# One core, attention over block sums with a residual layer norm: engine orders from a list schedule, and a projection of values

## The chip, the cores and the metric

The kernel runs on one core of a Trainium2 chip. The core has five engines, each with a queue of its own that it works through in order: TensorE (PE: matmuls; PEld: its weight loads), VectorE (DVE), ScalarE (ACT), GpSimd (POOL) and SyncE (SP, which here issues transfers). They meet only at semaphores. SBUF is the working memory of 128 partitions, PSUM the memory that TensorE writes; GpSimd has only operands in SBUF here. The metric is the time of one execution in microseconds; lower is better.

## The reference

`x` is 8 x 512 x 1024 in float32 (batch, sequence, hidden). The sequence of each batch is cut into 8 blocks of 64 rows.

```python
block_repr = inputs.reshape(B, n_blocks, block_size, H).sum(axis=2)
keys = jnp.einsum('bnh,kh->bnk', block_repr, Wk)
rms = jnp.sqrt(jnp.mean(keys * keys, axis=-1, keepdims=True) + EPS)
keys = keys / rms * rms_weight
scores = jnp.einsum('bnh,h->bn', keys, q)
attn = jax.nn.softmax(scores, axis=-1)
attended = jnp.einsum('bn,bnh->bh', attn, block_repr)
attended = jnp.broadcast_to(attended[:, None, :], (B, S, H))
proj = jnp.einsum('bsh,kh->bsk', attended, Wo)
x = inputs + proj
mu = jnp.mean(x, axis=-1, keepdims=True)
var = jnp.mean((x - mu) ** 2, axis=-1, keepdims=True)
out = (x - mu) / jnp.sqrt(var + EPS) * ln_gamma + ln_beta
...
x = x + _L0_cond_ref(...)
```

There are 8 x 8 blocks to attend over, one projected vector per batch, and then 4096 rows to be normalised and added to their input.

## The kernel before

**Tiles.** The 8 batches are taken as four groups of two (`GROUPS`). A group has 1024 rows of `x`, held as 8 "rows" of 128 x 1024 (one sequence row per partition), two to a tile of 1 MB, so that there are 32 rows `k` and 16 tiles in all. 13 tile buffers (`XBUFS`) hold `x` and, at first, the weights: SyncE issues group 0's four tiles, four of Wk, four of Wo, and then `x` tiles as buffers come free (L86, L95). TensorE transposes the weights into `wkT` and `woT` (L191), ScalarE and VectorE copying out in turn.

**The chain of a group.** `block_sums` (L222) adds the 64 rows of each block by matmuls with a 0/1 matrix; `to_columns` (L232) transposes the sums into `blkT`. `attend` (L246) makes the keys (`project`, L209: 64 instructions), their squares on ScalarE (L255) and dot products with the query on VectorE (L257), puts both into diagonal form (L260) and sums them over partitions (`pc`, L263). Some fifteen operations of 128 x 16 or 128 x 2 elements follow, nearly all in SBUF: the inverse root by an exponential of a logarithm and one Newton step (L276 to L278), the softmax (L279 to L290), and the weighted sum of the block columns (`att`, L294). `proj` (L300) then multiplies `att` by Wo (`po`, L214 again), adds gamma and beta as two further vectors, copies to `pr`, makes the table `tab` (L316, L319), and `spread_out` (L323) broadcasts the projection over the partitions into `pb` (L327), which has one PSUM buffer of two banks. All other steps of the chain share one PSUM buffer, `s1`.

**The rows.** `y_row` (L343): VectorE adds `pb` to the row in place and gets its sum (L351); ScalarE squares it and gets the sum of squares (L356). For each unit of four rows, `unit_std` (L361, ScalarE, two small operations), `unit_scale` (L368, VectorE, four operations of 128 x 4 elements, L373 to L376) and `unit_stat` (L379: GpSimd fills `stat`, L382; TensorE transposes it, L388; ScalarE copies it to `lt`, L392). `scale_row` (L395): ScalarE makes `A` = 1 + gamma x rs (L398, two buffers), GpSimd multiplies the row by it in place (L399); this document calls that a product. `rest_of_pair` (L401): TensorE makes for two rows what is still to be added, `b` (L411), from `lt` and `tab`. `out_of_pair` (L416): VectorE adds `b` (L420), and SyncE stores the tile and issues the next load.

**The order.** Every queue has the order in which the code emits. Group 0's chain comes first, with the weights' transposes. Then one loop runs over the rows `k`: `y_row(k)`, six rows behind it (`LAG`) `scale_row` and `rest_of_pair`, at each unit's end the unit's steps, eight rows behind `out_of_pair`; at the end of each turn the chains of the later groups, written as generators, are advanced by three pieces (`STEPS`). When a group's first row comes up, what is left of its chain is emitted at once.

## Time and profile before

| | us |
|---|---|
| median of three runs | 245.38 |
| lowest and highest run | 242.53, 247.69 |
| the profiled execution | 243.71 |
| its span in the trace | 241.8 |

The span runs from the first to the last instruction that the trace shows; the execution's own time is 1.9 us longer. The rows quoted below give start and duration in us from the span's start, the engine, the line (L) of the kernel, the output and input by name, and in brackets how long the engine had been idle and what released it. A granted clock (PEclk) of 1.00 is TensorE's level of 2.4 GHz, 0.50 that of 1.2 GHz.

### The profile page before, as it was taken

To read this page: it belongs to the slowest core of one execution; us is meant where nothing else is said; L and a number is where in the kernel's file an instruction comes from. 1 tells how busy PE (TensorE), PEld (TensorE's weight loads), DVE (VectorE), ACT (ScalarE), POOL (GpSimd) and SP (SyncE) were. 2 spreads that over 40 slices of the span, in tenths; PEclk is the share of its full clock that TensorE was granted. 3 is DMA by queue.
4 is the path that set the end of the run, shared out by engine and by line. 5 is a ranking of instruction groups with operands and counts; after the bars stand their busy time and mean duration, and the time that the engine had idled before them with its cause. 6 is when DMAs were issued, how large, how long until landed. Compare 5 with 4: busy or idle time off the path is not lost. (4 is left out here: it accounts for less than half of the span.)

```text
span 241.8 us, 2960 instructions
## 1 busy us (share of the span) xinstructions
PE 139.2 (58%) x1136; PEld 68.4 (28%) x1136; DVE 121.9 (50%) x209; ACT 97.1 (40%) x161; POOL 83.5 (35%) x75
## 2 busy tenths in 40 slices
PE   0677795986159609821578539801597065472970
PEld 0237674543123404301143313301144021211210
DVE  0004547064550154836990282737971595969542
ACT  0204324165370144642462232742371478482520
POOL 7300000000043043244325043433334439386990
PEclk9999999999556977965569756965569755555555
DMA  7999999899000003572454004120403034061664
GB/s 225 396 411 411 407 418 377 274 422 426 20 3 0 0 0 164 186 263 85 174 176 174 0 3 174 64 110 0 174 27 150 0 161 186 0 283 68 251 270 174
DMA packets 7342, 42.93 MB, mean 178 GB/s; under 512 B 792, under 2 KB 1056, under 8 KB 3232
## 3 DMA queue, kind: packets, MB, share of 16 engines
q1 hardware_dynamic: 6784, 41.95, 43.5%
q10 hardware_dynamic: 544, 0.80, 1.0%
q8 instruction: 9, 0.15, 0.2%
q14 instruction: 5, 0.04, 0.0%
HBM read 25.96 MB, written 16.78 MB: 177 GB/s over the span
## 5 line engine op out<-in xcount | busy, mean ns | idle before, releaser
L399 POOL TENSOR_TENSOR x<-x,A 128x1024 f32<-128x1024 f32 x32 | 74.8, 2356 | 94.2 <-ACT A L398 94.2
L351 DVE SCALAR_TENSOR_TENSOR x<-x,pb 128x1024 f32<-128x1024 f32 x32 | 38.2, 1214 | 37.4 <-PE pb L327 37.4
L356 ACT ACTIVATE sq<-x,ysum 128x1024 bf16<-128x1024 f32 x32 | 36.7, 1146 | 37.4 <-DVE x L351 30.6
L411 PE MATMUL b<-tab,lt 4*128 4x512 f32 x128 | 41.6, 949 | 12.6 <-DVE x L420 9.7
L420 DVE TENSOR_TENSOR x<-x,b 128x1024 f32<-128x1024 f32 x32 | 37.8, 1216 | 5.9 <-POOL x L399 4.8
L398 ACT ACTIVATE A<-gam,rs 128x1024 f32<-128x1024 f32 x32 | 36.3, 1137 | 4.0 <-POOL x L399 4.0
L388 PE MATMUL pl<-ident,stat 128*128 128x128 f32 x16 | 5.5, 448 | 50.2 <-POOL stat L382 50.2
L214 PE MATMUL po<-woT,att 128*32 128x256 f32 x256 | 21.5, 497 | 15.0 <-DVE att L294 15.0
L227 PE MATMUL bs<-x,blk 128*32 128x256 f32 x256 | 23.5, 526 | 10.2 <-DMA x<-in_x_dram 8.9
L373 DVE TENSOR_SCALAR ssq<-ssq 128x4 f32<-128x4 f32 x8 | 14.5, 1815 | 21.6 <-ACT r L364 21.6
L411 PEld LDWEIGHTS b<-tab,lt 4*128 4x128 f32 x128 | 12.4, 260 | 32.7 <-DVE x L420 22.0
L382 POOL TENSOR_TENSOR stat<-ysum,rs 128x8 f32<-128x8 f32 x8 | 1.7, 208 | 56.4 <-DVE rs L376 56.4
L214 PEld LDWEIGHTS po<-woT,att 128*32 128x32 f32 x256 | 10.2, 140 | 29.1 <-issue 24.0
L388 PEld LDWEIGHTS pl<-ident,stat 128*128 128x128 f32 x16 | 2.3, 204 | 56.0 <-POOL stat L382 56.0
L199 PE MATMUL pt<-ident,w 128*128 128x128 f32 x128 | 15.6, 275 | 2.5 <-DMA w<-in_L_cond_Wk_dram 1.9
L214 PE MATMUL keys<-wkT,blkT 128*32 128x256 f32 x256 | 15.1, 381 | 1.6 <-DVE blkT L242 1.6
L227 PEld LDWEIGHTS bs<-x,blk 128*32 128x32 f32 x256 | 9.6, 144 | 22.3 <-issue 6.9
L199 PEld LDWEIGHTS pt<-ident,w 128*128 128x128 f32 x128 | 13.9, 141 | 4.3 <-issue 3.0
L392 ACT COPY lt<-pl 128x256 f32<-128x256 f32 x8 | 3.0, 372 | 27.8 <-PE pl L388 27.8
L214 PEld LDWEIGHTS keys<-wkT,blkT 128*32 128x32 f32 x256 | 7.7, 110 | 8.4 <-DVE blkT L242 2.3
L242 DVE COPY blkT<-pblk 128x256 f32<-128x256 f32 x4 | 1.7, 425 | 15.8 <-PE pblk L239 15.8
L327 PE MATMUL pb<-pr,spread 128*128 128x256 f32 x32 | 8.7, 420 | 0.0
(69 smaller groups left out, 97.7 us busy)
## 6 DMA issues: line engine op xcount, KB each, us to landing
x<-in_x_dram SPq DMA_DIRECT2D x16, 1024.0 KB, 5.3
out_dram<-x SPq DMA_DIRECT2D x16, 1024.0 KB, 3.9
w<-in_L_cond_Wk_dram SPq DMA_DIRECT2D x4, 1024.0 KB
w<-in_L_cond_Wo_dram SPq DMA_DIRECT2D x4, 1024.0 KB, 17.7
gam<-in_L_cond_ln_gamma_dram ACTq DMA_DIRECT2D x1, 512.0 KB
qw<-in_cond_dram ACTq DMA_DIRECT2D x4, 32.0 KB, 3.6
w_t<-n_L_cond_rms_weight_dram ACTq DMA_DIRECT2D x4, 32.0 KB
gb<-in_L_cond_ln_gamma_dram ACTq DMA_DIRECT2D x4, 1.0 KB
```

The lines of the kernel that those rows point to most:

```text
L199: nc.tensor.transpose(pt[:, c, r * P : (r + 1) * P], stage[which, s][:, r, bass.ts(4 * h4 + c, P)], ident)
L214: nc.tensor.matmul(po[32 * j : 32 * j + 32, :], lhs(c), wT[:, c, bass.ts(j, QU)], start=(c == 0), stop=(end and c == HC - 1),)
L227: nc.tensor.matmul(G["bs"][32 * j : 32 * j + 32, :], blk[G["g"]], G["x"][t][:, r, bass.ts(j, QU)], start=(t == 0 and r == 0), stop=(t == G ...
L327: nc.tensor.matmul(pb[:, j, :], spread[G["g"]][:, j, :], G["pr"], start=True, stop=True)
L351: nc.vector.scalar_tensor_tensor(x_row(k), x_row(k), 1.0, place[k][0]["pb"], ALU.mult, ALU.add, accum_out=U["sum"][:, i : i + 1])
L356: nc.scalar.activation(junk, x_row(k), AF.Square, bias=U["sum"][:, i : i + 1], scale=-float(H), accum_out=U["ssq"][:, i : i + 1],)
L373: nc.vector.tensor_scalar(ssq, ssq, 1.0 / H**3, EPS, ALU.mult, ALU.add)
L388: nc.tensor.transpose(pl[:, k, :], st[:, RT * k : RT * k + RT].rearrange("p r i k -> p (r i k)"), ident)
L398: nc.scalar.activation(A, gam, AF.Identity, bias=1.0, scale=units[u]["rs"][:, i : i + 1])
L399: nc.gpsimd.tensor_tensor(x_row(k), x_row(k), A, ALU.mult)
L411: nc.tensor.matmul(bb[r][:, i, :], lt[lo : lo + K, :], G["tab"][lo : lo + K, :], start=True, stop=True)
L420: nc.vector.tensor_tensor(x_row(k + r), x_row(k + r), flat(bb[r]), ALU.add)
```

## The change

- **Order.** All work is entered as steps of a plan, each with its engine, an assumed cost, the steps it needs, a rank, and the buffer that it takes or gives back. When all are entered, `Plan.emit` lays them out in time: of all steps whose needs are laid out it takes the one that can start first (ties by rank, lower first), and at last emits all in the order of planned starts. Ranks are: loads -500, Wk transposes -300, small steps on TensorE for the rows -250, chains -200 + group, Wo transposes -199.8, a unit's small steps -150, rows by their number.
- **Units** have 2, 2, 4, 4, 4, 4, 4, 4, 2 and 2 rows. Small per-unit tiles have ten buffers.
- **Values.** The block columns themselves are multiplied by Wo (`values`, in the PSUM buffer `s2`, which the units' `pl` use too), which needs no softmax. The softmax's weights go into `w4` (ScalarE, 128 x 512) and, negative, into `stat`; `spread` multiplies `w4` by the values to make `pb`. `att`, `wb` and the addition over blocks on VectorE go. `b` takes 32 rows of `lt` and `tab` where it took four.
- **The softmax** keeps most of its small operands in the PSUM tile `pc`; the diagonal form on VectorE goes, `pc` being made from the broadcast sums and the diagonal matrix. The reciprocal keeps its operands in SBUF.
- **Units' small steps.** The inverse root (`e_scale`) moves from VectorE to GpSimd, as five operations; the copy to `lt` moves from ScalarE to VectorE.
- **Transfers.** gamma and beta are loaded early, on ScalarE's queue, in three transfers where there were nine. Constants made at the start change with the rest.

The core of the diff:

```diff
 XBUFS = 13
-LAG = 6
-STEPS = 3
+ABUFS = 2
+UNITS = (2, 2, 4, 4, 4, 4, 4, 4, 2, 2)
+class Plan:
+    def emit(self):
+        done, free, dma, start = {}, {}, 0.0, {}
+        pool = {kind: [0.0] * n for kind, n in self.buffers.items()}
+        left = list(range(len(self.steps)))
+        while left:
+            best = None
+            for i in left:
+                engine, cost, _, needs, rank, _, takes, _ = self.steps[i]
+                if any(n not in done for n in needs) or (takes and not pool[takes]):
+                    continue
+                at = free.get(engine, 0.0)
+                if takes:
+                    at = max(at, min(pool[takes]))
+                for n in needs:
+                    at = max(at, done[n] + (0.0 if self.steps[n][0] == engine else self.HOP))
+                if best is None or (at, rank, i) < best:
+                    best = (at, rank, i)
+            at, _, i = best
+            engine, cost, _, _, _, moved, takes, gives = self.steps[i]
+            free[engine] = done[i] = at + cost
+            if moved:
+                dma = max(dma, done[i]) + moved * self.MB
+                done[i] = dma + self.LAND
+            if takes:
+                pool[takes].remove(min(pool[takes]))
+            if gives:
+                pool[gives].append(done[i] + self.HOP)
+            start[i] = at
+            left.remove(i)
+        self.start, self.done = start, done
+        for i in sorted(start, key=lambda i: (start[i], i)):
+            self.steps[i][2]()
...
+    def load_x(G, t, needs):
+        def emit():
+            xx = xp.tile([P, RT, H], F32, tag="x", name=f"x{G['n']}_{t}")
+            nc.sync.dma_start(out=xx, in_=G["x_v"][t])
+            G["x"][t] = xx
+        G["loaded"][t] = plan.add(SP, 0.35, emit, needs, rank=-500 + len(loads), moved=1.0)
+        loads.append(G["loaded"][t])
...
+    def load_vectors():
+        for k, v in ((GAM, gamma), (BET, beta)):
+            dst = gb.rearrange("(j m) k -> j m k", m=32)
+            nc.scalar.dma_start(out=dst[:, k, :], in_=v.rearrange("(j k) -> j k", j=4))
+        nc.scalar.dma_start(out=gam, in_=gamma.rearrange("(o h) -> o h", o=1).to_broadcast([P, H]))
+    vectors = plan.add(ACT, 1.2, load_vectors, [staged[0, 0]], rank=-400)
...
+        def e_pc():
+            T["pc"] = ps.tile([P, 4, 32], F32, tag="s1", name=f"pc{n}")
+            for s in range(2):
+                nc.tensor.matmul(
+                    T["pc"][:, s, :], T["sd"][:, s : s + 1].to_broadcast([P, P]), diag4, start=True, stop=True
+                )
+        def e_ln():
+            T["r"] = row("cr")
+            nc.scalar.activation(T["r"], T["pc"][:, 0, :NB], AF.Ln, bias=eps_t, scale=1.0 / H)
+            nc.scalar.activation(T["r"], T["r"], AF.Exp, scale=-0.5)
+        def e_score():
+            r, pc = T["r"], T["pc"]
+            v, dot, t, a = (pc[:, i, :NB] for i in range(4))
+            nc.vector.scalar_tensor_tensor(t, v, H * EPS, r, ALU.add, ALU.mult)
+            nc.vector.scalar_tensor_tensor(a, t, -0.5 / H, r, ALU.mult, ALU.mult)
+            T["a"] = row("ca")
+            nc.vector.scalar_tensor_tensor(T["a"], a, 1.5, r, ALU.add, ALU.mult)
+            nc.vector.tensor_tensor(t, T["a"], dot, ALU.mult)
+            by = t.rearrange("p (b n) -> p b n", n=NBLK)
+            mx = small.tile([P, g], F32, tag=f"mx{g}", name=f"mx{n}")
+            nc.vector.tensor_reduce(mx, by, AX.X, ALU.max)
+            nc.vector.tensor_tensor(by, by, mx.unsqueeze(2).to_broadcast([P, g, NBLK]), ALU.subtract)
+        def e_exp():
+            nc.scalar.activation(T["pc"][:, 2, :NB], T["pc"][:, 2, :NB], AF.Exp)
...
+        def e_share():
+            sc = T["pc"][:, 2, :NB]
+            by = sc.rearrange("p (b n) -> p b n", n=NBLK)
+            es = small.tile([P, g], F32, tag=f"es{g}", name=f"es{n}")
+            nc.vector.tensor_reduce(es, by, AX.X, ALU.add)
+            nc.vector.reciprocal(es, es)
+            nc.vector.tensor_tensor(by, by, es.unsqueeze(2).to_broadcast([P, g, NBLK]), ALU.mult)
+            T["own"] = small.tile([P, 1], F32, tag="own", name=f"own{n}")
+            junk3 = row("junk3")
+            nc.vector.scalar_tensor_tensor(
+                junk3, sc, 1.0, diag4[:, :NB], ALU.mult, ALU.mult, accum_out=T["own"]
+            )
+        def e_stat0():
+            v = stat[n % 2].rearrange("p r i m -> p (r i) m")[:, :, :NB]
+            nc.vector.tensor_tensor(
+                v, T["pc"][:, 2, :NB].unsqueeze(1).to_broadcast([P, 2 * UNIT, NB]),
+                hide[g].rearrange("p b n -> p (b n)").unsqueeze(1).to_broadcast([P, 2 * UNIT, NB]), ALU.mult,
+            )
+        def e_w4():
+            T["w4"] = chain.tile([P, 4, P], F32, tag="w4", name=f"w4{n}")
+            nc.scalar.activation(flat(T["w4"]), flat(weigh[g]), AF.Identity, scale=T["own"])
+        i = plan.add(ACT, 0.6, e_sq, [keys], rank)
+        i = plan.add(DVE, 0.5, e_dot, [i], rank)
+        i = plan.add(PE, 0.4, e_pc, [i], rank)
+        i = plan.add(ACT, 0.45, e_ln, [i], rank)
+        i = plan.add(DVE, 1.2, e_score, [i], rank)
+        i = plan.add(ACT, 0.22, e_exp, [i], rank)
+        share = plan.add(DVE, 0.8, e_share, [i], rank)
+        G["stat0"] = plan.add(DVE, 0.3, e_stat0, [share, free.get(f"stat{n % 2}")], rank + 0.5, gives="s1")
+        w4 = plan.add(ACT, 0.59, e_w4, [share, free.get("w4")], rank)
+        T["values"] = {}
+        i = project(
+            rank + 0.5, columns, woT, "s2", f"values{n}", [blkT, *ready[1]], T["values"], False, "s2"
         )
-        yield
-
...
+        def e_spread():
+            pb = ps.tile([P, 4, QU], F32, tag="pb", name=f"pb{n}")
+            for j in range(4):
+                nc.tensor.matmul(pb[:, j, :], T["w4"][:, j, :], T["val"], start=True, stop=True)
+            G["pb"] = flat(pb)
...
+        i = plan.add(PE, 0.46, e_gb, [i, vectors], rank + 0.5)
+        free["blkT"] = i
+        val = plan.add(ACT, 0.37, e_val, [i, free.get("val")], rank + 0.5, gives="s2")
+        i = plan.add(PE, 1.1, e_ptab, [val], rank + 0.7, takes="s2")
+        G["tab"] = plan.add(ACT, 0.59, e_tab, [i, free.get(f"tab{n % 2}")], rank + 0.7, gives="s2")
+        G["spread"] = free["w4"] = free["val"] = plan.add(PE, 1.9, e_spread, [val, w4, *pb_free], rank)
...
+        def e_scale():
+            r0, ssq = U["r0"][:, :N], U["ssq"][:, :N]
+            a = unit.tile([P, UNIT], F32, tag="a", name=f"a{u}")[:, :N]
+            U["rs"] = unit.tile([P, UNIT], F32, tag="rs", name=f"rs{u}")
+            nc.gpsimd.tensor_scalar(ssq, ssq, 1.0 / H**3, EPS, ALU.mult, ALU.add)
+            nc.gpsimd.tensor_tensor(a, r0, r0, ALU.mult)
+            nc.gpsimd.tensor_tensor(a, a, ssq, ALU.mult)
+            nc.gpsimd.tensor_scalar(a, a, -0.5, 1.5, ALU.mult, ALU.add)
+            nc.gpsimd.tensor_tensor(U["rs"][:, :N], a, r0, ALU.mult)
+        def e_stat():
+            U["st"] = stat[G["n"] % 2]
+            nc.gpsimd.tensor_tensor(
+                U["st"][:, :N, :, GAM], U["sum"][:, :N].unsqueeze(2).to_broadcast([P, N, 2]),
+                U["rs"][:, :N].unsqueeze(2).to_broadcast([P, N, 2]), ALU.mult,
             )
...
+        std = plan.add(ACT, 0.48, e_std, squares, -150)
+        scale = plan.add(POOL, 1.0, e_scale, [std], -150)
+        i = plan.add(POOL, 0.2, e_stat, [scale, G["stat0"]], -150, takes=st_)
+        i = free[st_] = plan.add(PE, 0.35 * N // RT, e_pl, [i], -250, takes="s2", gives=st_)
+        lt = plan.add(DVE, 0.42, e_lt, [i], -150, takes="lt", gives="s2")
...
+                i = plan.add(ACT, 1.05, e_A, [scale], k, takes="A")
+                vs.append(plan.add(POOL, 2.36, e_v, [i], k, gives="A"))
...
+            bi = free[f"tab{G['n'] % 2}"] = plan.add(
+                PE, 1.5, e_b, [lt, G["tab"], *b_first], -250, takes="b", gives="lt" if end else None
             )
...
+            for k, v in zip(ks, vs):
+                def e_out(k=k, pair=pair):
+                    nc.vector.tensor_tensor(x_row(k), x_row(k), flat(U["b", pair][k % RT]), ALU.add)
+                i = plan.add(DVE, 1.14, e_out, [bi, v, i], k, gives="b" if k == ks[1] else None)
...
-    G0 = groups[0]
-    for t in range(G0["tiles"]):
-        block_sums(G0, t)
-    run(to_columns(G0))
-    for s in range(NW):
-        transpose_w(0, s)
-    transpose_w(1, 0)
-    first = attend(G0)
-    wo_at = {5: 1, 8: 2, 10: 3}
-    for n, _ in enumerate(first):
```

## Rows read from the trace of the kernel before

**Rows 1.** The page: its span, and part 1, busy time, share and instructions of each engine.
```profile
span 241.8 us, 2960 instructions
PE 139.2 (58%) x1136; PEld 68.4 (28%) x1136; DVE 121.9 (50%) x209; ACT 97.1 (40%) x161; POOL 83.5 (35%) x75
```

**Rows 2.** Stretches: from:to, length, PE, PEld, DVE, ACT, POOL busy (x), PEclk, DMA share, GB/s.
```profile
30.00:60.00 30.00, 23.64 (x324) 15.44 (x315) 13.44 (x33) 11.84 (x25) 0.00 (x0) 1.00 0.95 383
62.00:69.00 7.00, 0.21 (x1) 0.04 (x2) 4.72 (x18) 3.29 (x9) 0.00 (x0) 0.50 0.00 1
69.00:74.00 5.00, 4.99 (x40) 2.07 (x40) 0.99 (x2) 3.26 (x4) 3.92 (x2) 0.50 0.02 3
78.00:82.00 4.00, 2.83 (x30) 1.42 (x23) 0.00 (x0) 0.96 (x2) 0.00 (x0) 1.00 0.00 0
```

**Rows 3.** Timeline, first rows of groups: start, us, engine, line, out<-in, [idle before <-releaser].
```profile
49.37 1.22 DVE L351 SCALAR_TENSOR_TENSOR x<-x,pb 128x1024 f32<-128x1024 f32 x1 [7.74 <-PE pb L327]
83.68 1.22 DVE L351 SCALAR_TENSOR_TENSOR x<-x,pb 128x1024 f32<-128x1024 f32 x1 [13.68 <-PE pb L327]
87.36 2.34 POOL L399 TENSOR_TENSOR x<-x,A 128x1024 f32<-128x1024 f32 x1 [12.56 <-ACT A L398]
186.43 1.22 DVE L351 SCALAR_TENSOR_TENSOR x<-x,pb 128x1024 f32<-128x1024 f32 x1 [6.29 <-PE pb L327]
```

**Rows 4.** Groups by line and shape: busy us, mean ns | idle before, releaser.
```profile
L399 POOL TENSOR_TENSOR x<-x,A 128x1024 f32<-128x1024 f32 x32 | 74.8, 2356 | 94.2 <-ACT A L398 94.2
L373 DVE TENSOR_SCALAR ssq<-ssq 128x4 f32<-128x4 f32 x8 | 14.5, 1815 | 21.6 <-ACT r L364 21.6
L382 POOL TENSOR_TENSOR stat<-ysum,rs 128x8 f32<-128x8 f32 x8 | 1.7, 208 | 56.4 <-DVE rs L376 56.4
L276 DVE TENSOR_TENSOR ca<-cr 128x16 f32<-128x16 f32 x4 | 0.7, 170 | 1.7 <-ACT cr L274 1.7
L255 ACT ACTIVATE junk<-keys 128x256 f32<-128x256 f32 x4 | 1.5, 384 | 7.0 <-PE keys L214 7.0
```

**Rows 5.** Timeline, VectorE beside GpSimd, from 190 to 236 us.
```profile
190.10 2.34 POOL L399 TENSOR_TENSOR x<-x,A 128x1024 f32<-128x1024 f32 x1 [6.25 <-ACT A L398]
190.25 2.22 DVE L373 TENSOR_SCALAR ssq<-ssq 128x4 f32<-128x4 f32 x1 [2.58 <-ACT r L364]
214.35 6.96 POOL L399 TENSOR_TENSOR x<-x,A 128x1024 f32<-128x1024 f32 x3 [0.83 <-ACT A L398]
219.14 2.19 DVE L375 SCALAR_TENSOR_TENSOR a<-a,ssq 128x4 f32<-128x4 f32 x1
224.19 11.61 POOL L399 TENSOR_TENSOR x<-x,A 128x1024 f32<-128x1024 f32 x5 [2.28 <-ACT A L398]
226.58 1.22 DVE L420 TENSOR_TENSOR x<-x,b 128x1024 f32<-128x1024 f32 x1 [0.44 <-POOL x L399]
```

**Rows 6.** Timeline, VectorE and ScalarE back to back.
```profile
50.52 1.22 DVE L351 SCALAR_TENSOR_TENSOR x<-x,pb 128x1024 f32<-128x1024 f32 x1
50.64 1.15 ACT L356 ACTIVATE sq<-x,ysum 128x1024 bf16<-128x1024 f32 x1 [2.41 <-DVE x L351]
51.91 1.15 ACT L356 ACTIVATE sq<-x,ysum 128x1024 bf16<-128x1024 f32 x1
222.96 2.19 ACT L398 ACTIVATE A<-gam,rs 128x1024 f32<-128x1024 f32 x2
```

**Rows 7.** Timeline, TensorE: the steps around the projection, at either clock.
```profile
46.48 1.13 PE L316 MATMUL ptab<-pr,pick 128*128 128x256 f32 x4 [0.57 <-ACT pr L311]
47.45 1.89 PE L327 MATMUL pb<-pr,spread 128*128 128x256 f32 x8
54.42 3.66 PE L214 MATMUL keys<-wkT,blkT 128*32 128x256 f32 x64 [0.52 <-DVE blkT L242]
69.01 3.64 PE L214 MATMUL po<-woT,att 128*32 128x256 f32 x32 [6.80 <-DVE att L294]
180.34 1.14 PE L411 MATMUL b<-tab,lt 4*128 4x512 f32 x8
```

More of the change, by code (lines that the diff above doesn't have):

```diff
@@ new lines, in block_attn_resid_kernel @@
+    loads = []
+    for t in range(groups[0]["tiles"]):
+        load_x(groups[0], t, ())
+    for which in range(2):
+        for s in range(NW):
+            load_w(which, s)
+            loads.append(staged[which, s])
+    def load_vectors():
[3 more added lines that the diff above has]
+        nc.scalar.dma_start(out=gam, in_=gamma.rearrange("(o h) -> o h", o=1).to_broadcast([P, H]))
@@ L323, in spread_out @@
-    def spread_out(G):
-        pb = ps.tile([P, 4, QU], F32, tag="pb", name=f"pb{G['n']}")
-        for j in range(4):
-            nc.tensor.matmul(pb[:, j, :], spread[G["g"]][:, j, :], G["pr"], start=True, stop=True)
-        G["pb"] = flat(pb)
-    def run(steps):
-        for _ in steps:
-            pass
+        T = G["T"] = {}
+        rank = -200 + n
+        def row(name):
+            return small.tile([P, NB], F32, tag=f"{name}{g}", name=f"{name}{n}")
+        last = None
+        G["sums"] = []
@@ new lines, in attend, with sums @@
+        for t in range(G["tiles"]):
+            def sums(t=t):
+                if t == 0:
+                    T["bs"] = ps.tile([P, QU], F32, tag="s1", name=f"bs{n}")
+                for r in range(RT):
+                    for j in range(4):
+                        nc.tensor.matmul(
+                            T["bs"][32 * j : 32 * j + 32, :], blk[g], G["x"][t][:, r, bass.ts(j, QU)],
+                            start=(t == 0 and r == 0), stop=(t == G["tiles"] - 1 and r == RT - 1),
+                        )
+            last = plan.add(PE, 1.0, sums, [G["loaded"][t], last], rank, takes=None if t else "s1")
+            G["sums"].append(last)
@@ L336, in block_attn_resid_kernel @@
     NR = len(place)
-    units = {}
+    units, where = [], {}
+    for n in UNITS:
+        k0 = len(where)
+        for i in range(n):
+            where[k0 + i] = (len(units), i)
+        units.append(dict(k0=k0, n=n))
+    assert len(where) == NR
     def x_row(k):
@@ L416, in out_of_pair @@
-    def out_of_pair(k):
-        G, row = place[k]
-        bb = units[k // UNIT].pop(("b", k))
-        for r in range(RT):
-            nc.vector.tensor_tensor(x_row(k + r), x_row(k + r), flat(bb[r]), ALU.add)
-        t = row // RT
-        nc.sync.dma_start(out=G["out_v"][t], in_=G["x"][t])
-        if to_load:
-            load_x(to_load.pop(0))
-    G0 = groups[0]
-    for t in range(G0["tiles"]):
-        block_sums(G0, t)
-    run(to_columns(G0))
-    for s in range(NW):
-        transpose_w(0, s)
@@ L493, with load_next @@
+    to_load = [(G, t) for G in groups[1:] for t in range(G["tiles"])]
+    def load_next(needs):
+        load_x(*to_load.pop(0), needs)
+    for _ in range(XBUFS - len(loads)):
+        if to_load:
+            load_next([])
+    for f in frees:
+        if to_load:
+            load_next(f)
+    for G in groups:
+        attend(G)
+        for u, U in enumerate(units):
+            if place[U["k0"]][0] is G:
+                define_unit(u)
+    plan.emit()
+    return plan
 _INS = [
```

526 lines of the change are left out of this document (228 added, 298 removed).

## The prediction

> **What bounds the kernel now.** I read the page's busy shares first. No engine is busy for more than 58% of the 241.8 us [rows 1]; GpSimd, the least busy, works 83.5 us. So no engine sets the time as a whole, and the question is where they wait. The stretches by window come next. Until 60 us TensorE is busy 23.6 of 30 us at full clock and the loads run at 383 GB/s: this start is dense. From 62 us on there are long stretches in which nearly everything stands [rows 2]. The timeline says why. The first row of the output is begun on VectorE at 49.37 us; the first row of the next group only at 83.68 us, after 13.68 us in which VectorE waited for the broadcast projection `pb`; GpSimd got its next product at 87.36 us after 12.56 us idle. The fourth group begins at 186.43 us [rows 3]. So a group of 8 rows takes (186.43 - 49.37) / 3 = 45.7 us. Its rows need far less: GpSimd's 32 products take 74.8 us in all, 18.7 us for a group [rows 4]; back to back they take 11.61 / 5 = 2.32 us [rows 5]. VectorE's two operations on a row come 50.52 - 49.37 = 1.15 us apart, 2.3 us a row; ScalarE's square comes every 51.91 - 50.64 = 1.27 us, and its scaled gamma `A` takes 2.19 / 2 = 1.1 us, 2.4 us a row [rows 3, 6]. Three engines need about 2.3 to 2.4 us a row where the loop takes 5.7. What bounds the kernel is the order in the queues: each engine takes its work as the loop wrote it, and the attention of the next group advances three steps per row.
>
> A second loss shows in small operations. The 4-column `ssq` at 190.25 us took 2.22 us while GpSimd ran a product from 190.10; the 4-column `a` at 219.14 us took 2.19 us, up to the end of a product of GpSimd's [rows 5]. Such an operation takes 0.17 us alone [rows 4]. Meanwhile the wide add with `b` at 226.58 us took 1.22 us amid five products of GpSimd's [rows 5], as long as VectorE's other wide operation beside an idle GpSimd (50.52 us, [rows 6]). The first two have all operands in SBUF, the third reads PSUM.
>
> **The change part by part.** All sums are in the time of the profiled execution, 243.7 us outside a span of 241.8 us, 1.9 us apart; the median of the runs is 1.007 of that.
>
> *Start, to the first row.* Loads, transposes and the first chain stay. `spread` now precedes `ptab`, which gains the 0.97 us between their starts (46.48 and 47.45) [rows 7], and the projection by Wo no longer waits for the softmax. Against that, two tiles of block sums of the second group, whose loads come later, may stand ahead of the projection on TensorE, and the gamma vector, 0.5 MB, now loads among the weights. Bounds: 2 us sooner, 2 us later. I take no change, the first row at 49.4 us.
>
> *From the first row to the first product.* The first unit has two rows: 2.3 us on VectorE, 1.4 us for the last square, 0.5 us for two small ScalarE operations, then `scale`, now on GpSimd. No GpSimd operation of this shape, apart from `stat` at 0.208 us for 8 columns [rows 4], is in the trace. Five in a row, each waiting for the one before: I take 0.25 us each with a hand-over, 1.25 us, and 1.5 us with `stat`. The lower bound is 0.17 us each as on VectorE, 1.1 us for the unit; above, 0.7 us each, as if a three times dearer form, 4.4 us. Then `A`, 1.1 us. The first product is at 49.4 + 2.3 + 1.4 + 0.5 + 1.25 + 1.1 + hand-overs 0.2 = 56.2 us. The Trainium skill, GPSIMD Engine Reference, section "Engine selection", speaks against this move: elementwise work belongs on VectorE, GpSimd being about twice as slow with two inputs. By that rule five operations are 5 x 0.34 = 1.7 us, an estimate, and ten units would add some 5 us to the sum below. The trace's 0.208 against 0.17 us shows less than that.
>
> *What moves off VectorE and what it saves.* `ssq` in eight units cost 14.5 us before [rows 4]; gone from VectorE with three followers, they come back as about 1.5 us a unit on GpSimd, ten units, 15 us. GpSimd's total is then 32 x 2.32 + 15 = 89 us, and it becomes the fullest engine of the loop. VectorE's is 32 x 2.3 + ten copies of `lt` and three chains, some 87 us; ScalarE's much the same. The three are so level that a wait on any of them is seldom made up.
>
> *The softmax's small operations with an operand in PSUM.* They should keep 0.17 us beside a product, as the wide add did. One is left with all operands in SBUF, the reciprocal. It stands on the chain. Bounds: 0.17 us and 2.3 us, up to the end of a product. I take the middle, 1.2 us, as GpSimd will be working nearly always. The Trainium skill, SBUF — State Buffer, section "SBUF: two separate sides", says that a VectorE operation holds the port pair shared with GpSimd only in a two-port mode or with two SBUF inputs. The long `a`, which has two, agrees at 2.19 us. The reciprocal has one, and would wait only if it ran in such a mode; if not, three chains of the sum lose 1 us each.
>
> *The attention chain.* The weighted sum of values takes the projection by Wo off the way from softmax to `pb`. What is left: block sums 3.66 us (as `keys`), transposes 0.4, keys 3.66, the sums over a block 0.4, `spread` 1.89, TensorE 10.0 us at full clock [rows 7]; ScalarE six operations of at most 0.38 us [rows 4], 2.3 us; VectorE two of 0.45 us and ten of 0.2 us with their gap, 2.9 us; twelve hand-overs of 0.1 us. Bare: 16.4 us. Each step also meets an engine at work on rows: five visits to ScalarE at half an operation (0.6 us), four to VectorE (0.6 us), five to TensorE at half of 1.0 us, 7.9 us, and the reciprocal 1.2 us more. That makes 25.5 us. TensorE's clock: after a 7 us stretch with 0.2 us of work it stood at 0.50, remained there over 5 us of full work, and was at 1.00 by 78 us [rows 2]. At the low level 32 matmuls of `po` took 3.64 us where 64 of `keys` take 3.66 [rows 7]: exactly half. In the new order TensorE has per group 15.4 us of chain and values and four `b` of 1.14 us, in some 25 us; it should seldom stand long. I take a quarter of its chain cold: 2.5 us more, 28 us. Bounds: warm throughout 25.5, cold throughout 35.5 us.
>
> *The sum.* Each group's chain follows the last through one PSUM buffer (`s1`), freed some 3 us before `pb`. Group 1: 49.4 + 1.0 (`ptab`) + 28 = 78.4 us for its first row; four rows, square, `scale` and `A` later (4.6 + 1.4 + 0.5 + 1.25 + 1.1 + 0.1 = 8.9 us) its first product, at 87.3. Group 0's products end at 56.2 + 18.6 + two changes of unit with a wait for `A` (2 x 2.6) = 80.0 us, so GpSimd waits 7 us. Group 1's end at 87.3 + 18.6 + 1.5 = 107.4. Group 2: 75.4 + 28 = 103.4, first product 112.3, last done 132.4. Group 3: 100.4 + 28 = 128.4, 137.3, and with its two further units 137.3 + 18.6 + 3 = 158.9 us. Before, the span ended 6.0 us after GpSimd's last product (224.19 + 11.61 to 241.8) [rows 1, 5]; so 164.9 us, 166.8 outside the span, and 168 us against the median. The transfers need no term: the three late tiles of the last group load behind group 0's stores, some 40 us ahead of use, and a store of 1 MB per 5 us, some 210 GB/s, stays far under the 383 GB/s seen [rows 2].
>
> **The rivals.**
> *Cold TensorE.* Gaps between chain steps let the clock fall, as they did before. For it: the 0.50 in the window from 62 to 74 us. Against: far denser work. Each chain is 7.5 us longer, three chains 22 us: 190 us.
> *Dear small GpSimd operations.* At 0.7 us each, a unit costs 2.9 us more, ten units 29 us: about 197 us. For it: no row shows the operation. Against: `stat`'s 0.208 us.
> *The order doesn't come out as planned.* The list schedule counts on fixed costs; where one is off, an engine stands before an instruction whose input is late while others are ready. If half of a chain stays in the open, a group takes some 40 us: 49.4 + 3 x 40 + (8.9 + 21.6) + 6 + 1.9 = 208 us.
> *Slower.* One mechanism: on VectorE, in order, an add that awaits a product of GpSimd stands ahead of a chain step of the next group, so that no chain overlaps the products. A group is then 28 + 8.9 + 20.1 = 57 us, against 45.7 now, and the time 49.4 + 171 + 30.5 + 7.9 = 259 us. It is slower than before from 52 us a group on, when less than 5 us of the 28 are hidden. Against it: a step is emitted in order of its planned start, and an add is planned behind its product.
>
> **How the numbers follow.** Forecast 0.60: 168 us, from 152 to 178. Below, the chain is short enough that GpSimd never waits: 56.2 + 74.2 + 9 x 1.5 + 2.2 + 6.0 + 1.9 = 154 us, less up to 2 us at the start. Cold TensorE 0.17; dear GpSimd operations 0.08; order half lost 0.08; no change to speak of 0.03; slower 0.04. The range runs from 152 to 196 us, over the forecast, the cold clock and nearly all of the dear operations, some 0.83. Measured to about 2%, faster is 0.93, the same 0.03, slower 0.04.
>
> **What would show it.** Right: GpSimd's products come almost back to back from some 56 us on, with its idle time at the three group changes of 4 to 7 us; the softmax's operations at 0.2 us beside products; `scale` near 0.25 us each; TensorE's clock mostly at 1.00 until the last chain, some 130 us. Wrong: GpSimd idle for over 15 us before a group, with VectorE waiting for `pb`; a reciprocal or other small operation of 2 us at many places; a GpSimd `scale` above 0.5 us; a first row well after 51 us.

## The result and the profile after

The kernel takes 168.0 us, the median of 4 runs (166.18 to 168.85), where 245.4 us stood before: a ratio of 0.682 (95% interval 0.670 to 0.694). The forecast was 168.0 us. The profiled execution took 166.18 us outside a span of 164.3. Some executions on these chips are disturbed by about 1.5% and the comparison leaves them out; so the experiments are given below as medians of the undisturbed executions, and in that measure the kernel after stands at 166.7 us.

The total hides errors that cancel; that forecast and median are equal is luck. First the busy shares on the page after [rows 1], and the groups by line (busy us, mean ns; then the idle time before them and what ended it) [rows 4]:

```profile
span 164.3 us, 2996 instructions
PE 119.1 (72%) x1144; PEld 61.5 (37%) x1144; DVE 97.9 (60%) x175; ACT 97.0 (59%) x161; POOL 93.6 (57%) x124
```

```profile
L575 POOL TENSOR_TENSOR x<-x,A 128x1024 f32<-128x1024 f32 x32 | 75.0, 2370 | 10.7 <-ACT A L570 10.6
L597 DVE TENSOR_TENSOR x<-x,b 128x1024 f32<-128x1024 f32 x32 | 38.6, 1218 | 13.0 <-POOL x L575 10.8 <-PE b L585 2.0
L506 DVE SCALAR_TENSOR_TENSOR x<-x,pb 128x1024 f32<-128x1024 f32 x32 | 37.7, 1214 | 7.6 <-PE pb L454 7.6
```

The wide operations of VectorE, ScalarE and GpSimd cost what they did; VectorE's busy time fell from 121.9 to 97.9 us, all of it by its small operations. VectorE waited 7.6 us for `pb` in all (the first row alone), against 37.4 us for the same line before:

```profile
L351 DVE SCALAR_TENSOR_TENSOR x<-x,pb 128x1024 f32<-128x1024 f32 x32 | 38.2, 1214 | 37.4 <-PE pb L327 37.4
```

The timeline shows the same at the places of [rows 3]. The first row of each group on VectorE:

```profile
50.54 1.22 DVE L506 SCALAR_TENSOR_TENSOR x<-x,pb 128x1024 f32<-128x1024 f32 x1 [7.57 <-PE pb L454]
73.10 1.21 DVE L506 SCALAR_TENSOR_TENSOR x<-x,pb 128x1024 f32<-128x1024 f32 x1
99.23 1.21 DVE L506 SCALAR_TENSOR_TENSOR x<-x,pb 128x1024 f32<-128x1024 f32 x1
125.11 1.21 DVE L506 SCALAR_TENSOR_TENSOR x<-x,pb 128x1024 f32<-128x1024 f32 x1
```

The groups start 22.6, 26.1 and 25.9 us apart; before it was 45.7. On GpSimd, the timeline rows at which each group's products begin, and the last five:

```profile
57.49 4.71 POOL L575 TENSOR_TENSOR x<-x,A 128x1024 f32<-128x1024 f32 x2 [0.98 <-ACT A L570]
86.67 7.06 POOL L575 TENSOR_TENSOR x<-x,A 128x1024 f32<-128x1024 f32 x3 [0.99 <-ACT A L570]
110.47 4.73 POOL L575 TENSOR_TENSOR x<-x,A 128x1024 f32<-128x1024 f32 x2 [0.97 <-ACT A L570]
136.35 4.68 POOL L575 TENSOR_TENSOR x<-x,A 128x1024 f32<-128x1024 f32 x2 [0.97 <-ACT A L570]
146.60 11.59 POOL L575 TENSOR_TENSOR x<-x,A 128x1024 f32<-128x1024 f32 x5
```

GpSimd has no wait left as long as the 12.56 us of before; the longest is 3.38 us. Before its first product and at four of the nine changes of unit it waits 0.97 to 0.99 us for `A`, and that wait comes with the change itself: the five small operations stand behind the last product, and ScalarE can begin `A` only after them.

### The profile page after: what moved, and what is told of

Read it like the earlier page. It is cut to its first block, busy times and chain, and to the rows that moved or that the text cites. A ratio compares the mean times of both kernels' runs of the same rounds, so it can differ in the third digit from the quotient of the medians.

```text
span 164.3 us, 2996 instructions
## 1 busy us (share of the span) xinstructions
PE 119.1 (72%) x1144; PEld 61.5 (37%) x1144; DVE 97.9 (60%) x175; ACT 97.0 (59%) x161; POOL 93.6 (57%) x124
## 4 chain that ended last, share of the span: by engine, by line
PE 26%; POOL 21%; DVE 19%; DMA 17%; issue 7%; ACT 5%; POOLq 2%; ACTq 0%; SPq 0%; DVEq 0%
POOL x L575 17%; DMA w<-in_L_cond_Wo_dram 9%; DVE x L506 9%; PE keys L303 9%; DVE x L597 6%; PE values L303 6%; DMA x<-in_x_dram 5%; DMA qw<-in_cond_dram 3%; PE b L585 3%; PE pb L454 2%; PE pt L272 2%; ACT A L570 2%; ACT sq L514 2%; PE bs L330 2%; POOLq L653 1%
## 5 line engine op out<-in xcount | busy, mean ns | idle before, releaser
L575 POOL TENSOR_TENSOR x<-x,A 128x1024 f32<-128x1024 f32 x32 | 75.0, 2370 | 10.7 <-ACT A L570 10.6
L585 PE MATMUL b<-tab,lt 32*128 32x512 f32 x128 | 31.6, 794 | 8.3 <-DVE x L597 5.6
L330 PE MATMUL bs<-x,blk 128*32 128x256 f32 x256 | 19.7, 445 | 9.4 <-POOL pick L192 6.5
L303 PE MATMUL keys<-wkT,blkT 128*32 128x256 f32 x256 | 18.3, 435 | 2.8 <-DVE blkT L349 2.8
L585 PEld LDWEIGHTS b<-tab,lt 32*128 32x128 f32 x128 | 8.4, 221 | 21.6 <-DVE x L597 11.9
L303 PE MATMUL values<-woT,blkT 128*32 128x256 f32 x256 | 15.2, 381 | 0.0
L303 PEld LDWEIGHTS values<-woT,blkT 128*32 128x32 f32 x256 | 7.9, 110 | 5.7 <-issue 0.8
L279 DVE COPY wkT<-pt 128x1024 f32<-128x1024 f32 x4 | 4.9, 1225 | 6.4 <-PE pt L272 6.4
L279 ACT COPY wkT<-pt 128x1024 f32<-128x1024 f32 x4 | 4.1, 1013 | 7.4 <-PE pt L272 7.4
L454 PE MATMUL pb<-val,w 128*128 128x256 f32 x32 | 7.9, 389 | 0.7 <-ACT w L423 0.7
L556 DVE COPY lt<-pl 128x256 f32<-128x256 f32 (+1 forms) x10 | 3.7, 369 | 7.0 <-PE pl L549 7.0
```

Of the source, the lines that this page charges most:

```text
L279: (nc.vector.tensor_copy if n % 2 else nc.scalar.copy)(dst, hold["pt"])
L303: nc.tensor.matmul(hold["po"][32 * j : 32 * j + 32, :], lhs(c), wT[:, c, bass.ts(j, QU)], start=(c == 0), stop=(end and c == HC - 1),)
L330: nc.tensor.matmul(T["bs"][32 * j : 32 * j + 32, :], blk[g], G["x"][t][:, r, bass.ts(j, QU)], start=(t == 0 and r == 0), stop=(t == G["til ...
L454: nc.tensor.matmul(pb[:, j, :], T["w4"][:, j, :], T["val"], start=True, stop=True)
L575: nc.gpsimd.tensor_tensor(x_row(k), x_row(k), U.pop(("A", k)), ALU.mult)
L585: nc.tensor.matmul(U["b", pair][r][:, i, :], U["lt"][lo : lo + 32, pair, :], G["T"]["tab"][lo : lo + 32, :], start=True, stop=True,)
```

## The experiments

After the result there were two theories. One: GpSimd, nearly without a wait, sets the time. The other, the prediction's own: the attention chain through `s1` to `pb`, with the waits of its steps behind row work, sets the period of a group.

**GpSimd's own work, taken away.** In `a_no_scale` the five operations are gone and the exponential itself scales the rows (the Newton step is left out):

```
-        scale = plan.add(POOL, 1.0, e_scale, [std], -150)
+        scale = std
```

> The changed kernel without the five GpSimd operations of a unit (the Newton step of the inverse root is left out, rs is the exponential itself). Theory: GpSimd bounds the loop, being busy from its first scale to its last product but for short waits for A; ten units at 1.37 us fall away, 13.7 us, so 152 to 157 us. Rival, the chain up to pb still bounds: the three group starts don't move, 165 to 168 us. Half of the gain (159 to 163 us) would say that both are about level.

Measured: 163.5 us, 3.2 less, between the ranges. Ten times 1.37 us of GpSimd's time were taken away, 13.7 us, and most of it came back as waits. Two rows of its timeline (the profiled execution took 166.5 us), the first operations before a unit's products:

```profile
73.58 0.21 POOL L531 TENSOR_TENSOR stat<-ysum,r 128x8 f32<-128x8 f32 x1 [4.69 <-ACT r L527]
137.66 0.21 POOL L531 TENSOR_TENSOR stat<-ysum,r 128x8 f32<-128x8 f32 x1 [4.77 <-ACT r L527]
```

The second row opens group 3. The first stands inside group 0, before its last unit, whose squares ScalarE did only between steps of the next chain; so such a wait can also be for row work on ScalarE. GpSimd alone is not the bound. In `a_scale_dve` the inverse root goes back to VectorE, in SBUF:

```
-            nc.gpsimd.tensor_scalar(ssq, ssq, 1.0 / H**3, EPS, ALU.mult, ALU.add)
+            nc.vector.tensor_scalar(ssq, ssq, 1.0 / H**3, EPS, ALU.mult, ALU.add)
...
-        scale = plan.add(POOL, 1.0, e_scale, [std], -150)
+        scale = plan.add(DVE, 0.8, e_scale, [std], -150)
```

> The changed kernel with a unit's inverse root back on VectorE, four operations of 128x4 in SBUF, planned at 0.8 us. Theory: GpSimd loses 13.7 us of work, but two or three of the four operations stand until a product ends, some 4 us a unit on VectorE with the rows' additions behind them, on a path that leads to the next products: 168 to 178 us, no gain. Rival, the port costs nothing here and GpSimd's work alone counts: 154 to 158 us.

Measured: 166.4 us, no difference: no gain, as the theory said, but below its range. Its timeline (VectorE and GpSimd, one change of unit):

```profile
94.49 2.35 POOL L574 TENSOR_TENSOR x<-x,A 128x1024 f32<-128x1024 f32 x1 [0.46 <-ACT A L569]
94.54 2.33 DVE L533 TENSOR_SCALAR ssq<-ssq 128x4 f32<-128x4 f32 x1
96.78 0.15 DVE L534 TENSOR_TENSOR a<-r 128x4 f32<-128x4 f32 x1
96.97 0.16 DVE L535 SCALAR_TENSOR_TENSOR a<-a,ssq 128x4 f32<-128x4 f32 x1
```

At 94.54 the first of the four waits for the end of the product, as on GpSimd it waits in the queue behind it; at 141.18 the last one does. One of the four waited in four of the ten units (2.33 and 2.27 us long, twice about 1.0); in the other six all ran in 0.15 to 0.17 us, 0.19 us apart, where GpSimd needs 0.28. So these waits give back some 6 us, less than half of the 13.7 us that GpSimd loses. At the three group starts it now waited 0.96, 1.86 and 1.87 us for `rs`. As in `a_no_scale`, less work on GpSimd alone doesn't shorten the loop; which wait took each part is not shown.

**The same move alone, on the kernel before** (`b_scale_pool`: `unit_scale` in five operations of GpSimd, nothing else).

> Kernel before, with the inverse root of each unit (ssq, a, a, rs) on GpSimd in five operations, its order untouched. Before's groups by line show 14.5 us in ssq, most of it waiting for a product; on the chain to the next product this is some 1 us a unit net of the five GpSimd operations (about 1.4 us). Theory (order in the queues bounds before; small operations only lengthen a wait that is there anyway): 236 to 246 us. Rival (the waits of the small operations brought a large part of the gain): under 225 us.

Measured: 253.2 us, a ratio of 1.043 (1.031 to 1.056) to the kernel before: slower, outside both expectations; against the median of all executions of the kernel before beside it, 245.2 us, it is 8 us. The timeline of GpSimd at one change of unit, first in this kernel, then the row of the kernel before:

```profile
91.59 2.35 POOL L400 TENSOR_TENSOR x<-x,A 128x1024 f32<-128x1024 f32 x1 [14.65 <-ACT A L399]
...
95.42 0.21 POOL L383 TENSOR_TENSOR stat<-ysum,rs 128x8 f32<-128x8 f32 x1
```

```profile
90.26 0.21 POOL L382 TENSOR_TENSOR stat<-ysum,rs 128x8 f32<-128x8 f32 x1 [0.56 <-DVE rs L376]
```

From the product's end to the end of `stat` it is 95.63 - 93.94 = 1.69 us here and 90.47 - 89.70 = 0.77 us before (its product: [rows 3]). Here it is 0.92 us more; over the eight units of both timelines the same reading gives 0.5 to 1.1 us each, 6.7 us in all, of the 8 to 10 us between the medians (10 us from 243.2, the kernel before in the measure used here). So this edit of the change has a price of its own in the old order.

**The order.** `a_added_order` emits the same steps in the order in which they were added:

```
-        for i in sorted(start, key=lambda i: (start[i], i)):
+        for i in range(len(self.steps)):
```

> The changed kernel emitted in the order in which steps are added (a group's whole chain, then its units one after another), without the planned starts; all operations the same. Theory, the order is what brings the gain: no chain overlaps products and no unit overlaps the next; a group takes some 23 us of chain and 9 us to the first product and 20 us of products plus a like wait at each unit, 245 to 300 us. Rival, the cheaper operations bring most of it: under 215 us.

Measured: 284.3 us, a ratio of 1.158 (1.152 to 1.164) to the kernel before. Two of its first rows in the timeline, with the last add between them:

```profile
120.57 1.22 DVE L506 SCALAR_TENSOR_TENSOR x<-x,pb 128x1024 f32<-128x1024 f32 x1 [4.33 <-PE pb L454]
158.98 1.22 DVE L597 TENSOR_TENSOR x<-x,b 128x1024 f32<-128x1024 f32 x1 [1.09 <-POOL x L575]
178.10 1.22 DVE L506 SCALAR_TENSOR_TENSOR x<-x,pb 128x1024 f32<-128x1024 f32 x1 [4.33 <-PE pb L454]
```

This group takes 57.5 us, the others 62.4 and 56.1. So with the same operations this order costs 118 us more than the planned one (284.3 against 166.7); the loop order of the kernel before was not tried with the new operations. The other direction is `a_order_only`: the list schedule kept, and the inverse root, the softmax's operands and the late values undone at once (the edits of `a_scale_dve`, `a_softmax_sbuf` and `a_values_late` together).

> Kernel after with three of its edits undone at once: inverse root on VectorE in SBUF, softmax's small operations in SBUF, values product only after the softmax; what remains of the change is the list schedule (and the order of spread before ptab). Theory (the order brings nearly all; chain slope 0.77): values late +10.8 us, the small operations +5 to +9, the inverse root -1.6: 182 to 187 us, some 60 us under before. Rival (the edits need each other; VectorE's many small operations in SBUF wait and push the chain out of the rows' cover): over 195 us.

Measured: 190.1 us, here the median of all four executions (185.4 to 192.0), to be held against 245.4 and 168.0; it lies between the two ranges. By the shortest execution of each (185.4, 240.8, 166.2) the share is nearly the same. So what is left of the change without these three edits brings 55 of the 77 us, 70 to 75%. That is not the list schedule alone, as the expectation says: the smaller first and last units, the weights and values multiplied in `spread`, the sums `pc` without the diagonal form and the early gamma and beta are still in it. No run has the schedule by itself.

**The operations with an operand in PSUM.** `a_softmax_sbuf` puts the scores, exponentials and shares back into SBUF rows:

```
-            v, dot, t, a = (pc[:, i, :NB] for i in range(4))
+            v, dot = (pc[:, i, :NB] for i in range(2))
+            t, a = T["t"], T["a2"] = row("ct"), row("ca2")
```

> Kernel after, with the softmax's scores, exponentials and shares in SBUF rows again (the sums over a block stay in PSUM); nothing else changed. Theory (the chain through s1 to pb with its waits sets the period of a group): eight small VectorE operations of a chain have all operands in SBUF or two of them there; in the run with the inverse root on VectorE 4 of 40 such operations waited about 2.2 us, so of 8 x 4 here some 3 to 8 should wait, 1 to 2 in each chain on the path: three chains x 2 to 4 us x 0.77 gives +5 to +9 us, 173 to 177 us. Rival (these operations slip between products, or the port isn't shared by them): within 1.5 us of 168. The prediction's own view before (nearly every one waits for a product's end) would be +10 us a chain, over 190.

Measured: 177.4 us, 10.7 more, just over the theory's range. The groups by line on VectorE in this kernel:

```profile
L391 DVE SCALAR_TENSOR_TENSOR ca<-ca,cr 128x16 f32<-128x16 f32 x4 | 4.9, 1229 | 0.1
L407 DVE TENSOR_TENSOR ct<-ct,es 128x16 f32<-128x16 f32 x4 | 3.3, 813 | 0.1
L410 DVE SCALAR_TENSOR_TENSOR junk<-ct,diag 128x16 f32<-128x16 f32 x4 | 2.8, 697 | 0.2
L406 DVE RECIPROCAL es<-es 128x2 f32<-128x2 f32 x4 | 0.7, 166 | 0.1
```

Three operations with two SBUF inputs took 1.23, 0.81 and 0.70 us in the mean where in the kernel after they take 0.17 to 0.18: (1.05 + 0.63 + 0.52) x 4 = 8.8 us of waits on the chains, and 10.7 us of time. The timeline shows what they wait for:

```profile
93.35 4.70 POOL L576 TENSOR_TENSOR x<-x,A 128x1024 f32<-128x1024 f32 x2
95.29 0.47 DVE L389 SCALAR_TENSOR_TENSOR ca<-ct,cr 128x16 f32<-128x16 f32 x1
95.79 2.29 DVE L391 SCALAR_TENSOR_TENSOR ca<-ca,cr 128x16 f32<-128x16 f32 x1
```

Two products run from 93.35 to 98.05. `L389` ends where the first of them does, `L391` where the second does: such an operation gets in at the boundary between two products and not within one. Where no product ran, as at 130.78 and 130.99, `L407` and `L410` took 0.17 us here too.

**The chain, made longer and shorter.** `a_values_late` lets the projection of the values wait for the softmax; `a_half_keys` does half of the keys' product.

```
-            rank + 0.5, columns, woT, "s2", f"values{n}", [blkT, *ready[1]], T["values"], False, "s2"
+            rank + 0.5, columns, woT, "s2", f"values{n}", [blkT, share, *ready[1]], T["values"], False, "s2"
```

> The changed kernel with one more need: the projection of values waits for the softmax, as the projection by Wo did before. The operations are the same. The chain of groups 1 to 3 gets some 4.7 us longer (values 3.66, gamma and beta 0.63, copy 0.37). Theory, chains end just in time for GpSimd (it waited 0.7 and 0.4 us at two group starts): some of it shows, 171 to 177 us. Rival, the chain bounds: all three show, and the first group too, 180 to 186 us. If chains had slack: 168 to 170 us.

```
             def emit(c0=c0):
+                if end and c0 % 4:
+                    return
```

> Kernel after, with the keys product over half of the chunks of H (the other half left out), in each of the four groups: 1.8 us less of TensorE in each chain, no row operation touched and the plan laid out anew with the same costs listed. Theory (chain bounds, slope 0.77 from the run with the values late): the first chain 1.8 us and three more at 0.77 x 1.8 = 1.4 us: 4 to 6 us less, 162 to 164 us. Rival (the row work of an engine bounds from the first product on): only the first chain's 1.8 us, 166 to 168 us.

Measured: 178.2 us with the values late, 11.5 more, between the two ranges; 164.5 with half the keys, 2.2 less, where the chain theory expected 4 to 6. The 2.2 us are hardly more than executions of one kernel differ by (the two behind this median took 163.6 and 165.4). So a longer chain costs most of its length or more (8.8 us of waits in the softmax cost 10.7, four values products of some 4.3 us late cost 11.5), a chain that is shorter by 4 x 1.8 us gives 2.2 at most, and less work of GpSimd gave as little. That suggested a third theory: two limits at one height. GpSimd's is 57.5 + 75.0 + 9 x (1.58 + 0.98) = 155.5 us for its last product (1.58 us of small operations from 54.94 to 56.52, and the wait for `A`), measured 158.2. It is no floor: at three changes `A` stood ready and the change cost 1.6 us. The chain's limit must lie close to it, since GpSimd waits only 0.74 and 0.36 us at the last two group starts. Then both cuts together must give more than their sum (`a_both_cuts`, the two edits above):

> Kernel after with both cuts at once: the inverse root's five GpSimd operations left out (the exponential itself is used) and half of the keys product left out. Singly they gave 2.7 and 2.2 us. Theory (two limits stand level: GpSimd from its first product with a scale and a wait for A at each change of unit, 57.5 + 75.0 + 9 x 2.56 = 155.5 us against a last product's end measured at 158.2; and the chain through s1; taking one away uncovers the other at once): together more than the sum, 155 to 160 us, since GpSimd's limit falls by some 12 us and the chain's by 4 x 1.8 = 7 us. Rival (each cut works alone on its own share of waits): the sum of the two, 162.5 to 164 us.

Measured: 158.1 us, 8.6 less, where 3.2 + 2.2 = 5.4 would be the sum. Halving the keys leaves the plan's costs and so its order as they were; it gives 2.2 us beside the inverse root and 5.4 without it, so a new order is not what made the difference between these two. This fits the theory of level limits. But the 3.2 us beyond the sum rest on two or three executions of each kernel, up to 1.9 us apart, and with both cuts GpSimd still waited 3.19 and 3.35 us before two units: its own limit was not reached, and row work on ScalarE and VectorE (62% of that span each) was not tried as a third limit.

**A faster version.** `a_better1` leaves nothing out; `a_units` has the first line of it alone:

```
-UNITS = (2, 2, 4, 4, 4, 4, 4, 4, 2, 2)
+UNITS = (2, 2, 4, 4, 4, 4, 4, 4, 4)
...
-        scale = plan.add(POOL, 1.0, e_scale, [std], -150)
+        scale = plan.add(POOL, 1.37, e_scale, [std], -150)
...
-            nc.scalar.copy(T["val"], T["values"]["po"])
+            nc.vector.tensor_copy(T["val"], T["values"]["po"])
```

> Kernel after, made to be faster, nothing left out: the last group in units of 4 and 4 rows instead of 4, 2 and 2 (one change of unit less on GpSimd), the copy of the projected values on VectorE instead of ScalarE, and seven costs of the plan set to what the trace of after shows (inverse root 1.37, square 1.27, weights 0.72, b 1.2 us and the like). Theory of level limits: one change of unit less is 1.58 + 0.98 = 2.6 us off GpSimd's limit, the chain loses its stand behind A at one place (up to 0.6 us a group): 164 to 166 us. Rival (the tail after the last product grows by what the larger last unit holds back, or another order costs as much): 167 to 169 us.

> Kernel after with only the last group's units changed to 4 and 4 rows, all costs of the plan as in after. The first faster version had this, the copy of the values on VectorE and re-measured costs, and gave 6.7 us, where 2.6 us were expected of the unit. Theory (the change of unit is worth its 1.58 + 0.98 us and the rest came from the plan with true costs, in which the inverse roots come early enough for A to stand ready): 164.5 to 166.5 us. Rival (the unit alone brought it): 160 to 163 us.

Measured: 160.4 us for the first (ratio to the kernel before 0.657, 0.651 to 0.664), below both ranges; 165.1 us for the unit alone, within the theory's; 6.2 and 1.6 under the kernel after, and 1.6 us is about what executions of one kernel differ by. The rest, 4.6 us, lies in the plan's costs and the copy on VectorE, which were not tried apart. GpSimd's timeline in the first, from 107 us on:

```profile
107.13 7.04 POOL L575 TENSOR_TENSOR x<-x,A 128x1024 f32<-128x1024 f32 x3
114.25 0.20 POOL L533 TENSOR_SCALAR ssq<-ssq 128x4 f32<-128x4 f32 x1
...
115.81 11.77 POOL L575 TENSOR_TENSOR x<-x,A 128x1024 f32<-128x1024 f32 x5
```

Here the inverse root of the next unit stands between products of the one before; by the time it is needed `A` is there, and the 0.98 us are gone. From 98.40 us to the end of its last product at 151.83 GpSimd waits nowhere: for that stretch it is the limit. Before it, four waits for `A` make 5.1 us. A further version (`a_better2`: one of the five operations moved ahead, the dot product no longer behind the square, projections in eighths) came to 161.4 us:

> As the one before, and on both limits at once, nothing left out: the first of the inverse root's five operations goes ahead into a tile of its own, so that it needs only the squares (0.28 us less at a change of unit); the dot product with the query no longer waits for the sum of squares (about 0.5 us of each chain); projections laid out in eighths instead of quarters. Theory of level limits: 9 x 0.28 = 2.5 us off GpSimd's limit and 4 x 0.5 = 2 us off the chain, together 1 to 3 us below the run before, 161 to 165 us. Rival (the plan's order changes by chance at this scale and decides): within 2 us of the run before on either side.

The rival holds: the time is within 2 us of the run before. The plan laid its steps out in another order; in the profiled execution (164.3 us, longer than the median) GpSimd waited 3.02 us before a product at 89.11 that the first version had at 85.36. How much of the 1.0 us this explains is not shown.

## Why the prediction was right

**Start.** The first row came at 50.54 us, 49.4 predicted; the bounds of 2 us held, for reasons given with them. The last copy of `woT`, before and after, and the steps ahead of the values:

```profile
39.21 1.22 DVE L204 COPY woT<-pt 128x1024 f32<-128x1024 f32 x1
41.75 1.22 DVE L279 COPY woT<-pt 128x1024 f32<-128x1024 f32 x1
41.89 1.94 PE L330 MATMUL bs<-x,blk 128*32 128x256 f32 x32 [0.68 <-DVE stat L416]
43.64 3.64 PE L303 MATMUL values<-woT,blkT 128*32 128x256 f32 x64
```

The larger part is the weights: with gamma among the loads, the first transpose of Wo began at 29.89 us where it began at 27.56 before, and `woT` was complete at 42.97, 2.5 us later. That gamma's transfer alone did this is not shown. Two tiles of the next group's block sums stand ahead of the values and cost 0.6 us more. Against these stand the 0.97 us that `spread` gained and 1.2 us for which the projection had waited for the softmax before. First product 57.49, predicted 56.2: 1.3 us.

**The small GpSimd operations.** 0.19 to 0.20 us each, 0.28 from one to the next, 1.58 us with `stat`; predicted 0.25 and 1.5. They ran in 1.30 us without `stat` (54.94 to 56.23). The 1.7 us worked out by the Trainium skill, GPSIMD Engine Reference, section "Engine selection", took its factor of two for all five, while that section has it for two inputs only and GpSimd roughly at line rate with one; two of the five have one, so the rule makes 3 x 0.34 + 2 x 0.17 = 1.36 us, an estimate. Taken singly, the operations of the trace do not agree with the Trainium skill: beside 0.15 to 0.16 us on VectorE (`a_scale_dve`) 0.19 to 0.20 us is about a quarter more, not twice as much.

**What moved off VectorE.** The move of the inverse root, counted as a saving for VectorE, gained nothing: with it undone (`a_scale_dve`) the time is 0.3 us less.

**The softmax.** 0.17 to 0.18 us each beside products: right. The reciprocal was mis-sized, 1.2 us where it took 0.17 beside a product:

```profile
67.25 4.68 POOL L575 TENSOR_TENSOR x<-x,A 128x1024 f32<-128x1024 f32 x2 [3.38 <-ACT A L570]
68.81 0.17 DVE L405 RECIPROCAL es<-es 128x2 f32<-128x2 f32 x1
```

The Trainium skill, SBUF — State Buffer, section "SBUF: two separate sides", has two inputs in SBUF or a two-port mode as the condition. The trace agrees: the reciprocal, with one input, doesn't wait, and `L391` and `L407` with two do. `ssq` has one input and waited 2.33 us, which by that section of the Trainium skill makes it one of the two-port mode; no run here tried it apart.

**The chain and the first rows.** 78.4, 103.4 and 128.4 us predicted; 73.10, 99.23 and 125.11 measured. The step that failed is the start of the first of them: the sum lets group 1's chain begin after `ptab`, but three of its four tiles of block sums were done from 41.89 on, before the first row, and it came 5.3 us early. The three tiles, at 0.97 to 1.07 us each, are some 3 us of that; the rest is not taken apart.

The distance between the later groups, 25 us predicted, came at 26.1 and 25.9, in part by luck. From the time when `s1` is free (the end of `L416`) to the first row it is 29.6 us in group 2 and 31.1 in group 3, where 28 stood, and `s1` was free 3.5 and 5.3 us before the first row, where 3 stood. In the 28 us, next to nothing of the 2.5 us for a cold TensorE came in group 2 (granted clock 1.00 from 69.6 to 99.2 us), and 1.0 of the 1.2 us for the reciprocal did not. The waits behind other work were dearer: in group 2 the chain's own operations come to some 16 us, so that nearly 14 us are waits and hand-overs, where the sum had 7.9 + 1.2. Parts of this chain:

```profile
69.32 0.29 DVE L416 TENSOR_TENSOR stat<-pc,hide 128x128 f32<-128x128 f32 x1
81.67 3.66 PE L303 MATMUL keys<-wkT,blkT 128*32 128x256 f32 x64
84.31 1.15 ACT L514 ACTIVATE sq<-x,ysum 128x1024 bf16<-128x1024 f32 x1
85.45 1.14 ACT L570 ACTIVATE A<-gam,rs 128x1024 f32<-128x1024 f32 x1
86.50 0.36 ACT L363 ACTIVATE junk<-keys 128x256 bf16<-128x256 f32 x1
95.21 1.89 PE L454 MATMUL pb<-val,w 128*128 128x256 f32 x8
97.76 1.22 DVE L597 TENSOR_TENSOR x<-x,b 128x1024 f32<-128x1024 f32 x1 [2.54 <-POOL x L575]
```

The keys were ready at 85.33 (81.67 + 3.66). Their sum of squares began 1.17 us later: ScalarE, without a gap, finished a square and did a whole `A` first, where the sum had half an operation (0.6 us). At the chain's end `pb` was done at 97.10 (95.21 + 1.89), and the first row began only at 99.23: VectorE had stood idle for 2.54 us before an add that waits for a product of GpSimd, and did this add and a copy first. So a step of the chain waits through VectorE's queue for a product.

**GpSimd.** Predicted: products of group 0 done at 80.0, then waits of 7, 4.9 and 4.9 us at the three group changes, the sign given for being right. Measured: done at 84.0, and 0, 0.74 and 0.36 us before the small operations of the next group:

```profile
74.59 9.40 POOL L575 TENSOR_TENSOR x<-x,A 128x1024 f32<-128x1024 f32 x4 [0.98 <-ACT A L570]
84.07 0.19 POOL L533 TENSOR_SCALAR ssq<-ssq 128x4 f32<-128x4 f32 x1
107.89 0.19 POOL L533 TENSOR_SCALAR ssq<-ssq 128x4 f32<-128x4 f32 x1 [0.74 <-ACT r L526]
133.77 0.19 POOL L533 TENSOR_SCALAR ssq<-ssq 128x4 f32<-128x4 f32 x1 [0.36 <-ACT r L526]
```

So that sign did not come. Between the first and the last product the sum had 28.3 us beside the products, 17.1 of them at the group changes. Measured are some 25.7 us, 1.1 of them waits for a group; the changes of unit took the rest, 1.6 us where `A` stood ready, about 2.6 with the wait for it, and 5.0 and 3.7 us at two inside groups (waits of 3.38 us at 67.25, 2.05 at 124.06, not in the sum). The end fits: last product done at 158.2 (158.9 predicted), 6.1 us after it, 1.9 outside the span. The view that the chain bounds and GpSimd waits was half of it: both stand at about the same height. The prediction's sentence that VectorE, ScalarE and GpSimd are level came near this, without the conclusion that no single cut would help much.

**The clock.** The windows after (busy us and count of each engine, granted clock, DMA share, GB/s) [rows 2]:

```profile
56.00:80.00 24.00, 21.45 (x245) 10.53 (x238) 18.41 (x39) 20.15 (x37) 17.57 (x21) 0.93 0.46 174
87.00:107.00 20.00, 17.83 (x188) 8.94 (x188) 16.09 (x32) 16.85 (x27) 19.47 (x14) 1.00 0.63 233
112.00:132.00 20.00, 15.87 (x146) 7.40 (x138) 17.33 (x36) 16.14 (x28) 17.08 (x14) 0.89 0.34 138
137.00:158.00 21.00, 13.25 (x34) 3.39 (x34) 11.28 (x13) 11.39 (x17) 20.02 (x20) 0.50 0.44 182
```

At or near full clock for most of the time in which chains run (0.66 from 107 to 112 us), at half after the last, where only `b` is left: as said, and the cold rival falls.

**The slower rival** did not come. Its mechanism is there on a small scale, in the 2.54 us before the add above. `a_added_order` meets its price, 57 us a group, by other terms: 38.4 us from a group's first row to its last add (120.57 to 158.98), where the sum had 8.9 + 20.1 = 29.0, for there no unit overlaps the next either; and 19.1 us from there to the next first row, where it had a chain of 28. That the totals agree is chance; that an order without overlap is slower than before is shown.

## What to carry to other kernels

When the engines of a loop and the chain that feeds it are nearly level, cutting one gives little and lengthening one costs most of its length; cut both before you judge either. Where the order in the queues is the bound, look at the order before making operations cheaper: here the same operations took 284.3 or 166.7 us. The costs in a plan are best those of the trace, which together with one moved copy seems to have given 4.6 us. A small operation moved off a contended engine brings nothing if other waits take its place: the inverse root took the same time on VectorE and on GpSimd in the new order, and cost 8 to 10 us in the old.

## What the runs showed of the hardware

A small VectorE operation with two SBUF inputs that met a GpSimd product ended with it, 2.3 us at most, and got in at the boundary of two products (`a_softmax_sbuf`); with one operand in PSUM, or as a reciprocal with its one input, it took 0.17 to 0.18 us beside a product. GpSimd's operations of 2 to 8 columns cost 0.19 to 0.21 us.
